# Two layers of four-way row and column scans: other partitions for the row positions, other engines for moving rows to columns, another place for a square root, other first and last stages

## The chip, the cores and the metric

The kernel runs on one core of one Trainium2 chip. Its time is the device time of one execution in microseconds (us); the median of the runs of a kernel is compared. All data are 32-bit floats. The engines are TensorE (PE in the profile; PEld are its weight loads), VectorE (DVE), ScalarE (ACT), GpSimd (POOL) and SyncE (SP), which issues nearly all DMA transfers.

## The reference

```python
# x: (32, 48, 64, 128) = batch, channels, rows H, columns W; two layers, each with its own weights
x = x + conv(gn(x), down_w, down_b, right_w, right_b, left_w, left_b)

def gn(v):      # 16 groups of 3 channels; mean and variance over group, H and W of one batch element
    return (v - m) / sqrt(s + 1e-5)

def step(w, b):  # conv1d: 48 -> 48 channels, 5 taps, padding 2
    nxt = inp + conv1d(carry, w, b)

# conv(): four scans, each over the result of the one before it
# down : rows 0 .. 63,    carry = finished row, conv along W
# up   : rows 63 .. 0,    the same weights as down
# right: columns 0 .. 127, carry = finished column, conv along H
# left : columns 127 .. 0
```

Each step of a scan needs the finished step before it, so a scan is a chain of 63 row steps or 127 column steps.

## The kernel before, in words

**Passes.** The 32 batch elements are worked in four groups of eight, `g` = 0 to 3, and in two layers, which makes eight passes, `n` = 0 to 7 (layer 0 of all groups, then layer 1). Names end in layer and group and, for scans, in d, u, r or l: `row_02d` is the down scan of layer 0, group 2. One large on-chip buffer, `arena`, holds the state of a pass; `stage` is four smaller buffers of 112 x 2048 elements for data on their way. DRAM buffers `xin` and `mid` hold the input of the two layers in the kernel's own order, so `mid` is the result of layer 0.

**Two layouts.** For row scans (view `rows`) a column W = 8k + e is split in e (8 values) and k (16 values). The 8 x 48 = 384 pairs of e and channel lie in three blocks `o` of 128 partitions, and a row has 16 x 8 (k, batch) elements in each. `PIECES` lists, for each e, which channels `c0:c1` lie in which block from which partition `p0` on. For column scans (view `cols`) the 48 channels lie on partitions 0 to 47 for even rows and 64 to 111 for odd ones (`SIDES`), with 32 row pairs, e, k and batch in the free dimension. `cols` begins where row 20 of `rows` begins, so rows and columns share most of `arena`.

**Scans.** A row step (`row_step`, L523) is nine products in PSUM (`PRODUCTS`, weights `wd`) and, for each block, one VectorE addition of PSUM, bias and input row (L542). A column step (`col_step`, L546) is done in two halves of the batch, each of three matmuls (L556 to L560) and one VectorE addition (L563).

**From rows to columns.** While the up scan runs, `hand_over` (L415) moves finished rows to `cols`. `HANDS` says after which row which rows go: at 48, 32, 16, 8 and 0. Odd rows go first, then even ones, and each has twelve pieces, one DMA each, on SP's queue.

**Side work.** Other work is cut into portions that the program issues at certain scan steps (`advance`): writing out the results of the pass before with the residual added (`drain`, `residual`), loading (`load_rows`) and scaling (`scale_rows`, L411, ScalarE) the rows of the next pass, restaging the input of the next group (`prepare`: `take_in`, `restage`), and the statistics of the group norms. `input_moments` takes the next group's input in 16 portions, `result_moments` takes the layer-0 result of the pass before from `mid` in 16 parts of eight batch elements each. Both load into three buffers, `spare`, that lie in rows 0 to 15 of `arena`, so the next pass's first rows can be loaded there only when both are done. ScalarE does the sums: per portion the sums (L196), the negated mean (L199), the squares of the deviations (L201). `scaling` (L218) makes scale and offset of a group from them, with two small matmuls, about ten VectorE operations and a square root on ScalarE (L273).

**Order.** `dma()` (L145) keeps all of SP's transfers in program order. Within an engine the framework's scheduler fixes the order by its own estimates when the kernel is built; `behind_steps` (L210) makes the operations of `scaling` come after the instructions kept in `mark`, the last matmul and the last VectorE addition of the scan steps issued so far. Each engine then works in its fixed order, and an instruction that waits holds up those behind it.

**First and last stage.** `prepare_first` (L357) loads all input of group 0 in 16 tiles (`stage` and free parts of `arena`, whose partitions 32 to 63 are set to zero before), computes statistics with VectorE, restages each tile to `xin` and reads the rows back. `last_residual` (L472) writes the result of the last pass in four parts of k, each in four quarters of the rows: residual loads, eight additions (L504) and sixteen writes per quarter. A part can begin when the left scan has passed its columns.

## Time and profile before

| what | value |
|---|---|
| median of 3 runs | 5443.56 us (5439.95 to 5454.95) |
| profiled execution | 5430.74 us, span 5429.0 us |
| TensorE busy | 4811.6 us, 89% of the span |
| VectorE, ScalarE, GpSimd busy | 2527.8, 1850.8, 1013.8 us |
| mean granted TensorE clock | 0.95 |
| chain that ended last, by engine | PE 79%, ACT 7%, SP's issues 5%, DMA 5% |

The profile is of one execution, and its times are in us from the start of the span, mean times of one instruction in ns. In the strips over 40 slices each digit is the busy share of a slice of 135.7 us in tenths. A row of the waits names the waiting engine and instruction, then what it waited for: us in total, times, the longest. A row of the timeline has start, duration, engine, line, operation, what is written and read, the count of equal instructions, and in brackets how long the engine was idle ahead and what ended that. A row of groups has busy time, then the mean in ns, then idle time before.

### The profile page before, as it was taken

Reading aid. Unit: us, or ns where it says so; the run is one execution under the profiler, and the core shown is the slowest. Engines: PE = TensorE matmul, PEld = TensorE weight load, DVE = VectorE, ACT = ScalarE, POOL = GpSimd, SP = SyncE. Lnnn points to the kernel's source line nnn. Section 1 sums busy time; section 2 is a strip of 40 time slices with the busy share of each in tenths; the row PEclk is TensorE's granted clock in tenths of the full one; section 3 lists DMA queues with packets and bytes.
Section 4 is the critical chain, followed back from the end, with each engine's and each line's share of the span. In section 5 each row is a group of like instructions: output and inputs, shape, how many; then the busy total and the mean of one; then the engine's idle time right before and its main releaser. Section 6 shows DMA issues by size and latency. Waiting matters only on the chain.

```text
span 5429.0 us, 103969 instructions
## 1 busy us (share of the span) xinstructions
PE 4811.6 (89%) x42592; PEld 4802.6 (88%) x42592; DVE 2527.8 (47%) x7394; ACT 1850.8 (34%) x4090; POOL 1013.8 (19%) x409
## 2 busy tenths in 40 slices
PE   2799999899199896399999989998999989998992
PEld 2799999899199896398999989998999989998992
DVE  6344554455045453154554545554554445544553
ACT  3604043134970409831945079041004120050000
POOL 2103122130041210130003100260005300260044
PEclk9899999999599998699999999999999999999996
DMA  8569648881397943686338744288007840189057
GB/s 174 113 84 219 124 83 174 152 205 36 59 235 110 219 89 65 133 188 99 69 54 182 118 84 75 55 193 126 2 1 163 139 73 1 37 200 120 1 63 101
DMA packets 827086, 599.91 MB, mean 111 GB/s; under 512 B 246544, under 2 KB 763408, under 8 KB 822000
## 3 DMA queue, kind: packets, MB, share of 16 engines
q1 hardware_dynamic: 810720, 590.73, 57.2%
q8 instruction: 335, 5.49, 0.5%
q10 hardware_dynamic: 15888, 2.52, 0.3%
q14 instruction: 143, 1.17, 0.1%
HBM read 341.40 MB, written 151.09 MB: 91 GB/s over the span
## 4 chain that ended last, share of the span: by engine, by line
PE 79%; ACT 7%; SPq 5%; DMA 5%; POOL 1%; DVE 1%; issue 1%; ACTq 0%; DVEq 0%; POOLq 0%
SPq L147 5%; ACT arena L201 3%; ACT arena L196 3%; PE row_13d L534 2%; PE row_10d L534 2%; PE row_01d L534 2%; PE row_00u L534 2%; PE row_12d L534 2%; PE row_12u L534 2%; PE row_01u L534 2%; PE row_10u L534 2%; PE row_03u L534 2%; PE row_11u L534 2%; PE row_13u L534 2%; PE row_02u L534 2%; PE row_02d L534 2%
## 5 line engine op out<-in xcount | busy, mean ns | idle before, releaser
L411 ACT ACTIVATE arena<-arena,offset_m,scale_m 128x128 f32<-128x128 f32 (+1 forms) x864 | 422.0, 587 | 1246.9 <-DMA arena<-mid 835.9
L196 ACT ACTIVATE arena<-arena,sides 112x256 f32<-112x256 f32 (+1 forms) x560 | 475.9, 856 | 914.2 <-DVE arena L563 463.0
L456 POOL TENSOR_TENSOR stage<-arena,stage 112x1024 f32<-112x1024 f32 x96 | 361.0, 3793 | 1443.2 <-DVE arena L563 1368.7
L447 POOL TENSOR_TENSOR stage<-arena,stage 112x2048 f32<-112x2048 f32 x64 | 289.2, 4532 | 1442.1 <-DMA stage<-xin 801.4
L411 ACT ACTIVATE arena<-arena,offset_x,scale_x 128x128 f32<-128x128 f32 (+1 forms) x848 | 414.1, 586 | 164.1 <-DMA arena<-xin 95.6
L201 ACT ACTIVATE arena<-arena,neg_m 112x256 f32<-112x256 f32 x512 | 379.8, 749 | 0.7
L341 POOL COPY stage<-stage 112x1024 f32<-112x1024 f32 x98 | 196.7, 2036 | 744.3 <-DMA stage<-in_x 550.7
L534 PE MATMUL row_03d<-arena,wd 128*128 128x128 f32 x1134 | 133.7, 282 | 130.4 <-DMA arena<-xin 118.7
L534 PEld LDWEIGHTS row_03d<-arena,wd 128*128 128x128 f32 x1134 | 132.4, 198 | 131.8 <-ACT arena L411 122.4
L534 PE MATMUL row_02d<-arena,wd 128*128 128x128 f32 x1134 | 134.6, 283 | 128.8 <-DMA arena<-xin 118.8
L534 PEld LDWEIGHTS row_02d<-arena,wd 128*128 128x128 f32 x1134 | 133.2, 199 | 130.2 <-ACT arena L411 122.5
L534 PE MATMUL row_00d<-arena,wd 128*128 128x128 f32 x1134 | 136.8, 286 | 47.5 <-DVE arena L542 38.2
L534 PEld LDWEIGHTS row_00d<-arena,wd 128*128 128x128 f32 x1134 | 135.0, 201 | 49.2 <-DVE arena L542 43.2
L542 DVE SCALAR_TENSOR_TENSOR arena<-row_03d,bd,arena 128x128 f32<-128x128 f32 x189 | 61.3, 349 | 202.9 <-DMA arena<-xin 130.1
L542 DVE SCALAR_TENSOR_TENSOR arena<-row_02d,bd,arena 128x128 f32<-128x128 f32 x189 | 61.3, 349 | 202.1 <-DMA arena<-xin 131.2
L273 ACT ACTIVATE std_x<-var_x 128x24 f32<-128x24 f32 x4 | 0.9, 222 | 420.8 <-DVE var_x L268 420.8
L534 PE MATMUL row_11u<-arena,wd 128*128 128x128 f32 x1134 | 129.7, 277 | 7.1 <-DVE arena L542 7.1
L534 PEld LDWEIGHTS row_11u<-arena,wd 128*128 128x128 f32 x1134 | 128.7, 194 | 7.7 <-DVE arena L542 7.7
L563 DVE SCALAR_TENSOR_TENSOR arena<-col_02r,bc,arena 112x128 f32<-112x128 f32 x254 | 89.1, 351 | 99.1 <-PE col_02r L560 99.1
L563 DVE SCALAR_TENSOR_TENSOR arena<-col_01r,bc,arena 112x128 f32<-112x128 f32 x254 | 89.1, 351 | 98.1 <-PE col_01r L560 98.1
L563 DVE SCALAR_TENSOR_TENSOR arena<-col_13r,bc,arena 112x128 f32<-112x128 f32 x254 | 89.1, 351 | 98.1 <-PE col_13r L560 98.1
L563 DVE SCALAR_TENSOR_TENSOR arena<-col_12r,bc,arena 112x128 f32<-112x128 f32 x254 | 89.1, 351 | 97.9 <-PE col_12r L560 97.9
(231 smaller groups left out, 13835.2 us busy)
## 6 DMA issues: line engine op xcount, KB each, us to landing
arena<-arena SPq DMA_DIRECT2D x288, 192.0 KB, 7.5
xin<-stage SPq DMA_DIRECT2D x128, 384.0 KB, 6.2
stage<-xin SPq DMA_DIRECT2D x128, 384.0 KB, 8.2
mid<-stage SPq DMA_DIRECT2D x128, 384.0 KB, 5.8
arena<-mid SPq DMA_DIRECT2D x128, 384.0 KB, 6.1
arena<-in_x SPq DMA_DIRECT2D x124, 384.0 KB, 9.3
stage<-in_x SPq DMA_DIRECT2D x100, 384.0 KB, 11.2
stage<-mid SPq DMA_DIRECT2D x96, 384.0 KB, 6.9
```

Of the source, the lines that this page charges most:

```text
L147: tc.keep_in_program_order(nc.sync.dma_start(dst, src))
L196: nc.scalar.activation(view, view, AF.Identity, scale=sides, accum_out=mo.sum[:, b, t : t + 1])
L201: nc.scalar.activation(view, view, AF.Square, bias=mo.neg[:, b, t : t + 1], accum_out=mo.dev2[:, b, t : t + 1],)
L273: nc.scalar.activation(std, var, AF.Sqrt)
L341: nc.gpsimd.tensor_copy(dst[:, r], src[:, r])
L411: nc.scalar.activation(args[0], args[0], AF.Identity, bias=args[2], scale=args[1])
L447: nc.gpsimd.tensor_tensor(nat, res, nat, ALU.add)
L456: nc.gpsimd.tensor_tensor(perm[:, t].rearrange("p (b k e) -> p b k e", b=GB, k=NK), cols[:, q + t].rearrange("p e k b -> p b k e"), nat[:, ...
L534: mark["pe"] = nc.tensor.matmul(ps[o][:, a:b], wd[:, i, o - NG * s - i + 1], prev[:, i, a + s * GB : b + s * GB], start=seen[o] == 1, stop ...
L542: mark["dve"] = nc.vector.scalar_tensor_tensor(dst[:, o], ps[o], bd[:, layer, o : o + 1], inp[:, o], ALU.add, ALU.add).ins
L563: mark["dve"] = nc.vector.scalar_tensor_tensor(dst, ps, bc[:, layer, way : way + 1], dst, ALU.add, ALU.add).ins
```

## The change

Four things are changed.

- **Positions and hand-over.** `PIECES` is written out. In each block the two whole pieces of 48 channels start at partition 0 or 64 (e = 0, 1, 3, 4, 6, 7), and e = 2 and e = 5 are split in three pieces of 16 channels at partitions 48 and 112. `hand_over` moves whole pieces with a ScalarE copy and the 16-wide ones with a DMA, so a hand has 12 copies and 12 transfers. `HANDS` has one more hand: rows 4 to 7 and 0 to 3 go apart.
- **Square root and statistics.** `collect` keeps its last instruction in `mark["act"]`, so that `scaling`, its square root (now L285) among the rest, is placed behind statistics already issued. The statistics are asked for at every third step of the right scan up to step 50, where it was every fourth up to 65.
- **First stage.** Tiles lie elsewhere; less is set to zero ahead of the loads; four restage buffers; from the seventh tile on GpSimd restages both halves; row loads stand between the writes of `xin` on SP instead of behind them. The row weights are put together in a buffer and copied to `wd` by GpSimd, since the permuted positions break the runs in which they were written.
- **Last stage.** The residual loads of `last_residual` are issued from ScalarE's queue instead of SP's.

ScalarE in the right and left scans of pass 1, before (`sum_x`: sums of the next input; `sum_m`: of the result in `mid`; `std_x`: the square root for the next pass):

```order
L196 ACTIVATE arena,sum_x_7873<-arena,sides 112x2048
L199 ACTIVATE neg_x_7874<-sum_x_7873 112x1
L201 ACTIVATE arena,dev_x_7875<-arena,neg_x_7874 112x2048
L273 ACTIVATE std_x_9144<-var_x_9140 128x24
L196 ACTIVATE arena,sum_m_8656<-arena,sides 112x256 x8
L199 ACTIVATE neg_m_8657<-sum_m_8656 112x8
L201 ACTIVATE arena,dev_m_8658<-arena,neg_m_8657 112x256 x8
```

and now:

```order
L207 ACTIVATE arena,sum_m_8559<-arena,sides 112x256 x8
L210 ACTIVATE neg_m_8560<-sum_m_8559 112x8
L212 ACTIVATE arena,dev_m_8561<-arena,neg_m_8560 112x256 x8
L285 ACTIVATE std_x_9435<-var_x_9431 128x24
L207 ACTIVATE arena,sum_m_8559<-arena,sides 112x256 x8
```

The square root stood ahead of all sixteen result parts; now eleven of them are ahead of it and five behind.

VectorE at the same place, the operations of `scaling` that follow the square root, between the additions of the left scan (L563), before:

```order
L268 TENSOR_SCALAR var_x_9140<-ps_x_8918 128x24
L270 COPY mean_x_9142<-ps_x_8918 128x24
L563 SCALAR_TENSOR_TENSOR arena<-col_01l_10307,bc,arena 112x32x4
L278 RECIPROCAL r_x_9245<-std_x_9144 128x24
L280 TENSOR_TENSOR t_x_9247<-var_x_9140,r_x_9245 128x24
L563 SCALAR_TENSOR_TENSOR arena<-col_01l_10312,bc,arena 112x32x4
```

and now, where `col_01l_11195` is the last addition of the left scan and `row_02d` the first of the next pass:

```order
L579 SCALAR_TENSOR_TENSOR arena<-col_01l_11195,bc,arena 112x32x4
L290 RECIPROCAL r_x_9536<-std_x_9435 128x24
L292 TENSOR_TENSOR t_x_9538<-var_x_9431,r_x_9536 128x24
L294 TENSOR_TENSOR t_x_9540<-t_x_9538,r_x_9536 128x24
L298 TENSOR_SCALAR t_x_9582<-t_x_9540 128x24
L300 TENSOR_TENSOR scale_x_9584<-r_x_9536,t_x_9582 128x24
L302 SCALAR_TENSOR_TENSOR offset_x_9586<-mean_x_9433,scale_x_9584 128x24
L558 SCALAR_TENSOR_TENSOR arena<-row_02d_11200,bd,arena 128x128
```

The reciprocal and what follows it stood within the left scan and now stand between its last step and the first step of the next pass.

```diff
@@ -48,7 +48,7 @@
 SHIFT = 20
 CH = 2
 RB = 8
-HANDS = {48: 64, 32: 48, 16: 32, 8: 16, 0: 8}
+HANDS = {48: 64, 32: 48, 16: 32, 8: 16, 4: 8, 0: 4}
 DOWN, RIGHT, LEFT = range(3)
 
 LOADS = ((0, 4), (4, 12), (12, 20), (20, 28), (28, 36), (36, 44), (44, 52), (52, 60), (60, 64))
@@ -67,17 +67,22 @@
 )
 
 
-def pieces():
-
-    for e in range(E8):
-        lo = C * e
-        while lo < C * (e + 1):
-            hi = min(C * (e + 1), (lo // FULL + 1) * FULL)
-            yield e, lo - C * e, hi - C * e, lo // FULL, lo % FULL
-            lo = hi
-
-
-PIECES = tuple(pieces())
+
+
+PIECES = (
+    (0, 0, 48, 0, 0),
+    (1, 0, 48, 0, 64),
+    (2, 0, 16, 0, 48),
+    (2, 16, 32, 0, 112),
+    (2, 32, 48, 1, 48),
+    (3, 0, 48, 1, 0),
+    (4, 0, 48, 1, 64),
+    (5, 0, 16, 1, 112),
+    (5, 16, 32, 2, 48),
+    (5, 32, 48, 2, 112),
+    (6, 0, 48, 2, 0),
+    (7, 0, 48, 2, 64),
+)
 
 
 @with_exitstack
@@ -147,27 +152,33 @@
         tc.keep_in_program_order(nc.sync.dma_start(dst, src))
 
 
-    nc.gpsimd.memset(arena[32:64, H * ROW + 7 * CH * PAIR :], 0.0)
-    nc.vector.memset(stage[32:64], 0.0)
-    nc.gpsimd.memset(wd, 0.0)
     nc.vector.memset(sides, 1.0)
     nc.vector.memset(sides[32:64], 0.0)
     nc.vector.memset(sides[32:48], 1.0)
 
-    def load_row_weights(layer: int, queue):
+    def load_row_weights(layer: int, queue, eng, buf):
+
 
 
         for j in range(TAPS):
             d, si = divmod(TAPS - 1 - j, 2)
             queue(taps[layer][:, j], w[SIDES[si], layer, DOWN, d, SIDES[0]])
+        buf = buf[:, 0 : NG * NG * FULL].rearrange("p (i m) -> p i m", i=NG)
+        eng.memset(buf, 0.0)
         for e, c0, c1, i, p0 in PIECES:
             to = C * (e - TAPS // 2) - FULL * (i - 1)
             queue(
-                wd[p0 : p0 + c1 - c0, i].rearrange("p o m -> p (o m)")[
-                    :, to : to + TAPS * C
-                ],
+                buf[p0 : p0 + c1 - c0, i, to : to + TAPS * C],
                 taps[layer][c0:c1].rearrange("c k m -> c (k m)"),
             )
+        for i in range(NG):
+            for lin in range(NG):
+                for e, c0, c1, o, p0 in PIECES:
+                    if o == (lin + i - 1) % NG:
+                        at = FULL * lin + C * e + c0 - FULL * o
+                        eng.tensor_copy(
+                            wd[:, i, lin, p0 : p0 + c1 - c0], buf[:, i, at : at + c1 - c0]
+                        )
 
     def load_col_weights(layer: int, queue):
         queue(wc, w[:, layer, RIGHT : LEFT + 1])
@@ -205,6 +216,7 @@
                 bias=mo.neg[:, b, t : t + 1],
                 accum_out=mo.dev2[:, b, t : t + 1],
             )
+        mark["act"] = nc.cur_bb.bb.instructions[-1]
 
     @contextmanager
     def behind_steps():
@@ -331,11 +343,11 @@
 
     def restage(g: int, j: int, nat):
 
-        perm = stage[:, 2 + j % 2]
+        perm = stage[:, (2 + j) % 4 if g == 0 else 2 + j % 2]
         src = nat.rearrange("p (b r k e) -> p r e k b", b=GB, r=CH, e=E8)
         dst = perm.rearrange("p (r e k b) -> p r e k b", r=CH, e=E8, k=NK)
         for r in range(CH):
-            if g == 0 and r:
+            if g == 0 and r and j < 6:
                 nc.scalar.copy(dst[:, r], src[:, r])
             else:
                 nc.gpsimd.tensor_copy(dst[:, r], src[:, r])
@@ -360,23 +372,26 @@
         size = CH * PAIR
         tiles = [stage[:, 0], stage[:, 1]]
         for j in range(2, NCH):
-            at = H * ROW + size * (j - 2 if j < 9 else j - 16)
+            at = H * ROW + size * (j - 9)
             tiles.append(arena[0:P, at : at + size])
-            eng = nc.vector if j % 2 else nc.gpsimd
-            eng.memset(tiles[-1][32:64], 0.0)
         at = H * ROW + 7 * size
         st = arena[0:P, at : at + GB * NCH * 6].rearrange(
             "p (b j k) -> p b j k", b=GB, j=NCH
         )
+        nc.vector.memset(arena[32:64, at:], 0.0)
         for j, nat in enumerate(tiles):
+            eng = nc.vector if j % 2 else nc.gpsimd
+            eng.memset(nat[32:64], 0.0)
             take_in(0, j, nat)
+        nc.vector.memset(stage[32:64, 2:4], 0.0)
         for j, nat in enumerate(tiles):
             by_batch = nat.rearrange("p (b n) -> p b n", b=GB)
             for b in range(GB):
                 nc.vector.bn_stats(st[:, b, j, :], by_batch[:, b])
             restage(0, j, nat)
-            if j % 2 == 0 and j // 2 < EARLY:
+            if j % 2:
                 load_rows(0, 0, j // 2)
+        load_rows(0, 0, len(LOADS) - 1)
         mo = Moments(1, 1, "x0")
         mv = stat_tile(2 * GB, "mv", "x0").rearrange("p (b k) -> p b k", k=2)
         for b in range(GB):
@@ -387,8 +402,6 @@
         for _ in scaling(mo, 0, 0):
             pass
         for j in range(len(LOADS)):
-            if j >= EARLY:
-                load_rows(0, 0, j)
             scale_rows(0, 0, j)
 
     def load_rows(layer: int, g: int, j: int):
@@ -419,7 +432,10 @@
             src = rows[:, h0 + r : h1 : 2].rearrange("p q o n -> o p q n")
             dst = cols[SIDES[r], qs].rearrange("p q e k b -> e p q (k b)")
             for e, c0, c1, o, p0 in PIECES:
-                dma(dst[e][c0:c1], src[o][p0 : p0 + c1 - c0])
+                if c1 - c0 == C:
+                    nc.scalar.copy(dst[e], src[o][p0 : p0 + C])
+                else:
+                    dma(dst[e][c0:c1], src[o][p0 : p0 + c1 - c0])
 
 
 
@@ -481,7 +497,7 @@
             nat = inputs[half].rearrange("p (q e n) -> p q e n", q=nq, e=E8)
             for r in range(2):
                 for e in range(E8):
-                    dma(
+                    nc.scalar.dma_start(
                         nat[SIDES[r], :, e],
                         src[r, e][
                             :,
@@ -589,16 +605,13 @@
             yield "left", v
 
 
-    load_row_weights(0, nc.scalar.dma_start)
+    load_row_weights(0, nc.scalar.dma_start, nc.gpsimd, arena)
     load_col_weights(0, nc.scalar.dma_start)
     nc.scalar.dma_start(mask_sb, mask)
     nc.scalar.dma_start(bc, bias)
     for e, c0, c1, o, p0 in PIECES:
         nc.scalar.dma_start(bd[p0 : p0 + c1 - c0, :, o], bias[c0:c1, :, DOWN])
-    nc.scalar.dma_start(
-        maskp.rearrange("p o m -> p (o m)").rearrange("p (e c) -> p e c", e=E8),
-        mask[:, 0:C].unsqueeze(1).to_broadcast([P, E8, C]),
-    )
+        nc.gpsimd.tensor_copy(maskp[:, o, p0 : p0 + c1 - c0], mask_sb[:, c0:c1])
     prepare_first()
 
     side = {}
@@ -650,10 +663,10 @@
                         side["prepare"] = prepare(nxt[1])
                     side["moments"] = all_moments(n)
                     if nxt and nxt[0] != layer:
-                        load_row_weights(nxt[0], dma)
+                        load_row_weights(nxt[0], dma, nc.gpsimd, arena)
                 if i % 6 == 2:
                     advance("prepare")
-                if i % 4 == 2 and i < 66 and n + 1 < NGRP:
+                if i % 3 == 2 and i <= 50 and n + 1 < NGRP:
                     advance("moments")
                 elif i % 8 == 2:
                     advance("moments")
```

## The prediction

> **What bounds the kernel now.** I read the page first, for how much of the span PE works and where it does not; then PE's waits, which give the price of each hole; then what releases the three kinds of holes.
>
> ```profile
> PE 4811.6 (89%) x42592; PEld 4802.6 (88%) x42592; DVE 2527.8 (47%) x7394; ACT 1850.8 (34%) x4090; POOL 1013.8 (19%) x409
> PE   2799999899199896399999989998999989998992
> ACT  3604043134970409831945079041004120050000
> PE row_02d L534 <- DMA arena<-xin: 118.8, 1, 118.8
> PE row_03d L534 <- DMA arena<-xin: 118.7, 1, 118.7
> PE col_01r L556 <- DMA arena<-arena: 15.0, 1, 15.0
> PE col_03r L556 <- DMA arena<-arena: 13.4, 1, 13.4
> 273.48 126.66 PE row_00u L534 x1134
> 1026.47 0.74 PE L556 MATMUL col_01r<-arena,wc 112*112 112x128 f32 x2 [15.03 <-DMA arena<-arena]
> 1369.64 0.38 PE L560 MATMUL col_01l<-arena,wc 112*112 112x124 f32 x2
> ```
>
> The span is 5429.0 us, the profiled execution took 5430.74. TensorE is at 9 tenths nearly everywhere: the scans are a serial chain of matmul and VectorE addition, and a step costs 126.66/63 = 2.01 us in the row scans and (1370.02 - 1026.47)/254 = 1.35 us in the column scans. Neither step is touched, so the change can only move the holes. There are four kinds: the start (the first slice reads 2), the end (the last reads 2), two boundaries of 119 us (the 1s and 3s in the middle; passes 1 to 2 and 2 to 3), and eight hand-overs, of which the longest and the shortest wait are shown.
>
> **The boundaries.** Here is what ScalarE does in pass 1, between the first column step (call it R = 1026.47) and the next pass:
>
> ```profile
> ACT std_x L273 <- DVE var_x L268: 420.8, 4, 122.2
> 1167.37 0.19 ACT L201 ACTIVATION_READ_ACCUMULATOR arena<-arena,neg_x 112x1 f32 x1
> 1289.76 0.22 ACT L273 ACTIVATE std_x<-var_x 128x24 f32<-128x24 f32 x1 [122.20 <-DVE var_x L268]
> 1289.89 0.75 ACT L196 ACTIVATE arena<-arena,sides 112x256 f32<-112x256 f32 x1
> 1482.27 0.19 ACT L201 ACTIVATION_READ_ACCUMULATOR arena<-arena,neg_m 112x1 f32 x1
> 1488.81 1.22 PE L534 MATMUL row_02d<-arena,wd 128*128 128x128 f32 x4 [118.79 <-DMA arena<-xin]
> 1546.16 87.28 PE row_02d L534 x766
> 2387.16 8.05 PE row_03u L534 x72
> ```
>
> Input statistics end at 1167.56, which is R+141. The square root is next in ScalarE's queue, and its operand comes 122.20 us later. Behind it stand sixteen parts of result statistics, 1289.89 to 1482.46, 192.6 us or 12.04 each. The left scan has ended at 1370.02, 112 us before them. The first rows of the next pass share the statistics' buffers, so their loads come last.
>
> The change puts that square root after 11 of the 16 parts and asks for the statistics every third step, not every fourth. ScalarE then has no reason to stand still. Even if the input statistics do not end sooner, the results run from R+141, plus some 7 us for their first load, for 192.6 us: to R+341, against the scan's end at R+343.5. The hole as such closes. What is late next: the reciprocal and the five operations behind it now stand on VectorE after the last left step, so no scaling of the next rows can start before; then the first rows must be scaled.
>
> ```profile
> L411 ACT ACTIVATE arena<-arena,offset_x,scale_x 128x64 f32<-128x64 f32 x24 | 9.5, 489 | 3.1 <-DMA arena<-xin 3.1
> L411 ACT ACTIVATE arena<-arena,offset_x,scale_x 128x128 f32<-128x128 f32 x30 | 15.4, 614 | 0.0
> ```
>
> Six operations of some 0.3 us make 2 us; the first four rows take 9.5 us; the next eight 24 x 0.51 = 12.3, less four row steps of 2.01 that run meanwhile: 2 + 9.5 + 12.3 - 8.0 = 16, and 2 for the cold start, 18 in all. Before, a boundary cost 118.8 and then a down scan of 1633.44 - 1488.81 = 144.6 instead of 126.7, together 136.7 (the other one likewise). Gain 2 x 119 = 238. Bounds: at the top 246, if the scalings pipeline by 4 us more; at the bottom 118, if each part waits for its loads on SP behind the restaging of the next input, 16 us a part instead of 12.04, so 16 x 4 less a little, 60 us late per boundary. A row for such waits is there, for the input parts:
>
> ```profile
> ACT arena L196 <- DMA arena<-in_x: 318.5, 31, 182.0
> ```
>
> **The hand-overs.** Row results go to the column layout by 24 transfers per hand, all issued by SP.
>
> ```profile
> L147 SPq DMA_DIRECT2D arena<-arena x25: 582/602/615, 1013.7 to 1029.6; - x25
> DMA to landing us min/median/max: 2.0/2.3/2.6
> L201 ACT ACTIVATE arena<-arena,neg_x 112x2048 f32<-112x2048 f32 x48 | 96.1, 2003 | 1.6
> L201 ACT ACTIVATE arena<-arena,neg_m 112x256 f32<-112x256 f32 x512 | 379.8, 749 | 0.7
> L339 ACT COPY stage<-arena 112x1024 f32<-112x1024 f32 x14 | 28.1, 2020 | 15.4 <-DMA xin<-stage 15.4
> ```
>
> 25 issues in 15.9 us are one per 0.66: the last hand takes 24 x 0.66 = 15.8 us, and that, less the issues for the odd rows that begin before the last row ends and with a landing behind it, is the wait of 13.4 to 15.0 us that PE shows. Now 12 of the 24 are ScalarE copies. SP needs 12 x 0.66 = 7.9 us, and the piece that the second column step reads (the third of the even rows) is issued at 8 x 0.66 = 5.3 and lands at 7.6; the step before it, which reads only copied columns, is done by then: hole about 6.3. The copies have no row here. In the last hand each has 256 elements a partition: 250 ns by the widest statistics row (2003 x 256/2048), 505 by the one kind of copy that ScalarE makes now, with strided operands (2020 x 256/1024), 749 by the row of the same size; twelve make 3.0, 6.1 or 9.0 us. I take the middle, since that row is a copy; the first column needs only two of the twelve, so the copies lie beside SP's issues. Gain 8 x (14.1 - 6.3) = 62. Bounds: 96 if the hole is 2 us, one landing; 16 if copies and pieces together keep it at 12. The 72 copies of a pass (36 of 1024 elements, 12 of 512, 24 of 256) make 97 us by the copy row, beside an up scan of 126.7 in which PE waits for nothing of ScalarE's.
>
> **The start.**
>
> ```profile
> 0.00:18.00 18.00, 0.00 (x0) 0.00 (x0) 13.79 (x8) 0.00 (x0) 15.15 (x14) 1.00 0.47 87
> 18.00:79.00 61.00, 0.00 (x0) 0.00 (x0) 46.14 (x125) 6.61 (x4) 3.73 (x2) 1.00 1.09 209
> 95.00:137.00 42.00, 34.54 (x261) 33.68 (x262) 13.66 (x42) 36.04 (x54) 12.06 (x6) 0.88 0.70 178
> 137.00:185.00 48.00, 13.75 (x110) 12.97 (x108) 5.85 (x18) 26.84 (x33) 14.06 (x7) 0.67 0.92 201
> 2.51 6.88 DVE L151 MEMSET stage<- 32x8192 f32 x1 [2.51 <-issue]
> 94.93 10.29 PE L534 MATMUL row_00d<-arena,wd 128*128 128x128 f32 x72 [5.72 <-POOL arena L409]
> ```
>
> (Columns after the length: PE, PEld, DVE, ACT, POOL busy, PE clock, DMA share, GB/s.) Input loads run at full DMA share from 18 to 79 us; before 18 they stand at 0.47, behind memsets of the tiles they fill, of which the first takes 6.88. With memsets a quarter as long ahead of them they are full from about 5: 0.47 x 18 + 1.09 x 61 = 75 us of transfers, at 1.09 in 69 us, so they end 9 or 10 us sooner, and everything up to the first matmul with them. The first down scan runs from 94.93 to 273.48, 178.6 us, of which 51.9 are not steps; 42 of them lie between 95 and 185, where rows wait behind 22 writes of restaged input on SP. With reads interleaved they wait only for ScalarE's scalings: 24 x 0.61 = 14.7 us for eight rows against 16.1 of steps, so 12 us remain, mostly the first rows. Gain 10 + 40 = 50; bounds 20 (in the first loads nothing, half of the stall) and 58.
>
> **The end.**
>
> ```profile
> 5203.31 16.49 POOL L504 TENSOR_TENSOR stage<-arena 112x256 f32<-112x256 f32 x16 [316.76 <-DVE arena L563]
> 5211.60 9.09 SPq L147 DMA_DIRECT2D out<-stage  x16
> 5331.10 0.37 PE L560 MATMUL col_13l<-arena,wc 112*112 112x124 f32 x2
> 5374.09 15.29 SPq L147 DMA_DIRECT2D stage<-mid  x16
> 5389.43 37.07 SPq L147 DMA_DIRECT2D out<-stage  x48
> L504 DVE TENSOR_TENSOR stage<-arena x10: 601/1483/1491, 5374.1 to 5404.9; 112x256 f32<-112x256 f32 x10
> q1 hardware_dynamic: 164864, 20.47, 72.3%
> q10 hardware_dynamic: 12800, 1.57, 4.6%
> ```
>
> PE ends at 5331.5 and the span 97.5 us later: SP has fallen behind, since it issues the loads of residuals too. These go to ScalarE's queue, which is idle there. Then a quarter part costs SP 9.1 us of writes and POOL 16.49/2 = 8.25 us of additions; four of them take some 37 us, and the left scan frees a part in 32 x 1.35 = 43, so parts 3 to 1 are done with the scan. Behind it lies part 0: four quarters at five VectorE additions of 1.48, 30 us, and the last writes, 5 to 12: a tail of 42. Gain 55; bounds 12 (one part still late by a whole cycle of 43) and 68.
>
> By the Trainium skill ("DMA: Bandwidth & Descriptors", section "Issuing engines are not separate DMA queues") all issuers share the same 16 DMA engines, and a second issuer saves only the time of issue, usually little. The trace does not refute it; by it the gain of this part could be near zero, which is the first rival.
>
> **The sum.** 238 + 62 + 50 + 55 = 405 off 5430.7 gives 5026 for a profiled execution. The median of the runs shown, 5443.56, lies 12.8 above the profiled one; I add that: **5040**. At all lower bounds, 118 + 16 + 20 + 12 = 166, it is 5278; at all upper, 468, it is 4976.
>
> **The rivals.**
>
> 1. *The DMA engines bound the end* (15%). Over the 226 us from 5203 the two queues' packets took 72.3 + 4.6 = 76.9% of 16 engines, 174 us. Starting at 5211.6 they could not end before 5386: tail 54, time 5052; with the whole of today's tail kept, 5095. For it: the share is high for a stage in which SP issues one transfer after the other. Against it: it is not 1, so the engines have room that the issuing leaves.
> 2. *The small pieces keep the hand-over late* (12%). Twelve DMAs still follow the last row, and a landing of 2.3 us comes after the last that matters; if the wait ends with the last one and copies slow it, the hole is 12: 5040 + 8 x 5.8 = 5086.
> 3. *Result statistics are paced by SP* (10%). They start early but their loads stand behind the input's restaging: 60 us late at both boundaries, 5040 + 120 = 5160.
> 4. *The other side: result statistics without overlap* (3%). The results share three buffers and SP's queue with the restaging of the next input. If each load waits until the part before is done and SP has gone through the restaging, a part costs load and work one after the other. At 26 us a part (12.04 of work, and some 14 of waiting, against the 318.5/31 = 10.3 of the input row) they end at R+141+7+416 = R+564, 220 behind the scan; with the 18 that makes 238 a boundary, 102 more than now, and the loss of 204 exceeds the other three gains (167): 5443 + 37 = 5480. It decides from 25 us a part on. For it: 31 waits of input parts in the row above. Against it: while the results run now, back to back, a part takes 12.04, and the earlier request leaves SP more steps ahead of them.
>
> That the change does not do what it says is excluded for the square root: the order of ScalarE shows it behind eleven parts.
>
> **How the numbers follow.** The forecast has 60%, the rivals 15, 12, 10 and 3. The range 4980 to 5140 holds the forecast's own spread (boundaries 8 up, hand-overs 34 up, start and end some 20 either way), rivals 1 and 2, and leaves out the third and the fourth and both tails. A measurement of this kernel tells 0.3%, 16 us, from no change. All cases but the fourth are far on the faster side: faster 0.95, same 0.02, slower 0.03.
>
> **What would show it.** PE's waits for xin at row_02d and row_03d should be under 25 us instead of 119, and std_x should wait on ScalarE for little; what holds PE there should be ScalarE's scalings or the offset of VectorE. Waits at the col_..r steps should be near 6 us, eight times. PE should start near 85 and the first down scan should end near 224. PE's end should lie some 42 us before the span's end, with POOL never idle for over 5 us in it before part 0. Wrong would be: result statistics on ScalarE that end after the left scan, by waits for DMA arena<-mid; col waits of 12 and more; a last stage in which DMA share stays at 0.9 while SP idles.

## The result

The changed kernel takes 5083.43 us (median of 4 runs, 5067.92 to 5099.47); the kernel before takes 5441.76 (median of 4 runs). The ratio is 0.934, 95% interval 0.930 to 0.937: 358 us or 6.6% faster. Forecast were 5040 and a range of 4980 to 5140. The sign, the range and the largest term held; 43 us of the forecast gain did not come.

### The profile page after: what moved, and what is told of

The parts are those of the page before. It is cut to its first block, busy times and chain, and to the rows that moved or that the text cites. A ratio compares the mean times of both kernels' runs of the same rounds, so it can differ in the third digit from the quotient of the medians.

```text
span 5072.3 us, 104799 instructions
## 1 busy us (share of the span) xinstructions
PE 4806.6 (95%) x42592; PEld 4794.2 (95%) x42592; DVE 2534.4 (50%) x7396; ACT 2272.9 (45%) x4656; POOL 1049.0 (21%) x504
## 5 line engine op out<-in xcount | busy, mean ns | idle before, releaser
L436 ACT COPY arena<-arena 48x1024 f32<-48x1024 f32 (+2 forms) x576 | 437.1, 759 | 767.8 <-DVE arena L558 760.7
L579 DVE SCALAR_TENSOR_TENSOR arena<-col_11r,bc,arena 112x128 f32<-112x128 f32 x254 | 89.0, 351 | 87.7 <-PE col_11r L576 84.4
L579 DVE SCALAR_TENSOR_TENSOR arena<-col_03r,bc,arena 112x128 f32<-112x128 f32 x254 | 89.0, 351 | 86.7 <-PE col_03r L576 83.0
L520 POOL TENSOR_TENSOR stage<-arena 112x256 f32<-112x256 f32 x54 | 58.3, 1118 | 356.6 <-DVE arena L579 328.4
```

What stands on the lines that cost most here:

```text
L436: nc.scalar.copy(dst[e], src[o][p0 : p0 + C])
L520: eng.tensor_tensor(perm[:, :, t].rearrange("p b (k e) -> p b k e", k=kn), cols[:, no * i + t, :, ks].rearrange("p e k b -> p b k e"), nat ...
L579: mark["dve"] = nc.vector.scalar_tensor_tensor(dst, ps, bc[:, layer, way : way + 1], dst, ALU.add, ALU.add).ins
```

## The profile after, stage by stage

The engines' busy times and two strips of the page of the changed kernel (span 5072.3 us, execution 5074.23):

```profile
PE 4806.6 (95%) x42592; PEld 4794.2 (95%) x42592; DVE 2534.4 (50%) x7396; ACT 2272.9 (45%) x4656; POOL 1049.0 (21%) x504
PE   1999999999999999999999999999999999998994
ACT  2645214489735897359453891533005510143000
```

TensorE's work is the same, and it now fills 95% of the span: the two dips in the middle of its strip are gone. Of what PE waited for, the rows that the change bears on (us in total, times, longest):

```profile
PE col_13r L572 <- DMA arena<-arena: 17.5, 1, 17.5
PE row_02d L550 <- ACT arena L424: 8.1, 3, 5.1
PE row_03d L550 <- ACT arena L424: 8.0, 3, 5.0
PE col_02r L572 <- DMA arena<-arena: 3.0, 1, 3.0
PE col_12r L572 <- ACT arena L436: 0.5, 1, 0.5
```

The two waits of 119 us are down to 8, and behind them now stand ScalarE's scalings. In pass 1 ScalarE has its last result part done at 1284.44, 28 us before the left scan ends, and then itself waits for the coefficients:

```profile
ACT arena L424 <- DVE offset_x L302: 30.2, 1, 30.2
```

The hand-overs' waits are 3 us, but one of 17.5 has come in the last pass that was in no forecast. From the first and last matmul of each scan:

| stage, us | before | after | gain | forecast |
|---|---|---|---|---|
| first matmul | 94.9 | 106.1 | -11 | 10 |
| first down scan beyond its 126.8 | 51.7 | 6.5 | 45 | 40 |
| eight hand-overs: holes and right scans | 1496.0 | 1419.0 | 77 | 62 |
| boundaries 1 to 2 and 2 to 3 | 274 | 38 | 236 | 238 |
| last matmul to the end of the span | 97.5 | 69.7 | 28 | 55 |

A boundary is its hole, the excess of the down scan behind it over 126.8 and that of the left scan ahead of it over 171.5: before 136.6 + 137.4 = 274, after 17.0 + 15.3 + 5.7 = 38. These gains are 375 us; the spans differ by 357. The other 18 lie mostly in row scans of layer 1: 8 in the up scan of pass 5 (137.4 before, 145.6 after), which took 147.3 in a second profile of the kernel before and so differs by execution, and some 3 in each of the down scans of passes 5 to 7, for which no cause is shown.

## Experiments

Every run but one is the changed kernel with the edit shown. Beside them the kernel before took 5454.6 to 5458.5 us (medians), 13 to 17 more than beside the changed kernel, so between them and the changed kernel's 5083.43 a difference of some 15 us says nothing by itself; the holes in the profiles say more.

**The boundaries: which half of the edit closed them?** Two runs undo one half each.

```diff
-        mark["act"] = nc.cur_bb.bb.instructions[-1]        # e1_mark_undone
-                if i % 3 == 2 and i <= 50 and n + 1 < NGRP:  # e1_pace_undone
+                if i % 4 == 2 and i < 66 and n + 1 < NGRP:
```

> The square root is put back ahead of the sixteen result parts on ScalarE; statistics still asked for at every third step. Theory (both halves are needed: the place of the root and the earlier request, which moves the root's operand on VectorE from left half-step 134 to 52): ScalarE stands still from the end of the input statistics (about R+141, R being the first column step) to left half-step 52 (R+172+35 = R+207), then works 192.6 us, to R+400, 56 us behind the left scan; with what follows (24 us before) each of the two boundaries costs some 80 us instead of 17 to 21: 120 us more in all, about 5200. Rival 1 (the place of the root alone closed the hole): 136 us a boundary as before, 235 more, 5318. Rival 2 (the earlier request alone closed it): no change, 5083.

> Statistics asked for at every fourth step again; the root still goes behind statistics already issued, which now are five result parts, and its operand comes at left half-step 129. Theory: ScalarE does five parts, waits until about R+172+87 = R+259, then does eleven parts of 12.04, to R+392, 48 us behind the scan; boundaries of some 72 us, 105 more in all, about 5190. Rival 1 (the place of the root alone closed the hole): no change, 5083. Rival 2 (the request alone): as before the change, 5318.

Measured: 5215.99 us (5210.72 to 5221.27) with the mark undone, 5218.83 (5216.92 to 5220.75) with the pace undone: 133 and 135 above the changed kernel, where 120 and 105 were expected and the rivals said 0 and 235. ScalarE's wait for the root in pass 1 and PE's holes, with the mark undone:

```profile
ACT std_x L284 <- DVE var_x L279: 92.6, 1, 92.6
PE row_02d L549 <- DMA arena<-xin: 67.3, 1, 67.3
PE row_03d L549 <- DMA arena<-xin: 67.2, 1, 67.2
```

and with the pace undone:

```profile
ACT std_x L285 <- DVE var_x L280: 41.0, 1, 41.0
PE row_02d L550 <- DMA arena<-xin: 55.2, 1, 55.2
PE row_03d L550 <- DMA arena<-xin: 55.1, 1, 55.1
```

In the changed kernel std_x waits for nothing in this pass. So neither half does it alone: the earlier request moves the root's operand from left half-step (half of a column step) 134 to 52, and the mark lets ScalarE work meanwhile. A third run asks whether the root stands too late, since the coefficients now come behind the last left step. It is taken from a kernel whose first residual loads are on SP (below).

```diff
-        mark["act"] = nc.cur_bb.bb.instructions[-1]
+        if mo.T == 2 or t < 5:     # behind five result parts
+            mark["act"] = nc.cur_bb.bb.instructions[-1]
```

> As the run with only the first residual loads on SP, and the square root of passes 1 and 2 is placed behind five result parts, not eleven. Its operand comes at left half-step 52 (R+207), when ScalarE has just done five parts (R+148+60), so it stands nowhere; reciprocal to offset then lie at left half-step 154 instead of behind the last step. Theory (what is left of a boundary is the coefficients behind the scan and the scaling of the first rows behind them, and VectorE's small operations take 4.4 us each where GpSimd's additions have begun): the result parts still end at R+325, the first rows can be scaled before the scan ends at R+345, the waits of 5 to 22 us at row_02d and row_03d and the slow first steps behind them go: 15 to 17 us per boundary, 30 to 50 in all: 5071 - 35 = 5036, with less spread between runs. Rival (the loads of the first rows end last, not the coefficients): boundaries stay at 15 us, 5071.

Measured: 5094.84 us (5080.79 to 5097.21), against 5071.11 for its base: slower than theory and rival had it. PE waits for the loads of the first rows, as the rival said. The run's waits in pass 1 and at the row scan:

```profile
ACT std_x L286 <- DVE var_x L281: 28.6, 1, 28.6
PE row_02d L552 <- DMA arena<-xin: 6.5, 1, 6.5
```

ScalarE had done five parts some 24 us sooner than I reckoned (the earlier request shortened the input statistics too), stood 28.6 us before the root, and so ended the results with the scan (1315.97 and 1316.36) instead of 28 us before it as in the changed kernel; the first rows' loads come behind that. The hole with the down scan behind it costs 6.5 + 149.1 - 126.8 = 29 us, not 17 to 19. An estimate from these numbers: the root would stand well behind seven or eight parts (28.6/12.04 = 2.4 more); that was not tried.

**The hand-overs.** All pieces by SP, new positions and hands kept:

```diff
-                if c1 - c0 == C:
-                    nc.scalar.copy(dst[e], src[o][p0 : p0 + C])
-                else:
-                    dma(dst[e][c0:c1], src[o][p0 : p0 + c1 - c0])
+                dma(dst[e][c0:c1], src[o][p0 : p0 + c1 - c0])
```

> All twelve pieces of a hand go by SP again, from the new positions and with the extra hand at row 4. Theory (SP's 24 issues of 0.66 us set the hole, whatever the hand's size): 13 to 15 us before the second or third column step at seven passes instead of the 3 us that are left now, and more in the last pass, where SP's issues are late already: 8 x 11 = 88, and some 10 for the last pass: about 5180. Rival (the smaller last hand made the gain): holes stay near 3 us, 5085.

Measured: 5311.53 us (5304.73 to 5316.71), 228 more than the changed kernel. PE's longest and shortest wait of the eight, and two between:

```profile
PE col_13r L569 <- DMA arena<-arena: 45.3, 1, 45.3
PE col_01r L569 <- DMA arena<-arena: 34.2, 1, 34.2
PE col_00r L569 <- DMA arena<-arena: 33.0, 1, 33.0
PE col_10r L569 <- DMA arena<-arena: 31.6, 1, 31.6
```

The copies are what closes the hole, as the theory said, but its size was wrong: I had 14 us from the last hand alone, and SP carries a backlog. SP's hand-over transfers of pass 1, first in the kernel before, up to the end of the last row (1011.45) and from there to the first column step, then the same in this run (1000.42):

```profile
912.52 99.11 SPq L147 DMA_DIRECT2D arena<-arena  x72
1011.02 15.90 SPq L147 DMA_DIRECT2D arena<-arena  x24
```

```profile
901.47 99.03 SPq L152 DMA_DIRECT2D arena<-arena  x84
999.89 35.17 SPq L152 DMA_DIRECT2D arena<-arena  x53
```

The kernel before has ten pieces for odd and ten for even rows, since e = 2 and e = 5 are split in two; with five hands a pass has 100 transfers. 72 are out when the last row ends, and the first column step waits for the 91st: 19 issues of 0.66 and a landing of 2.6 make its 15 us. In this run a pass has 144, twelve pieces and six hands; 84 are out, and the step waits for the 133rd: 49 issues and a landing of 2.0, 34 us. So without the copies the new positions and the extra hand are a loss; which of the two costs more, no run tells. With the copies a pass has 72 transfers, 63 of them out when the last row ends, and SP just keeps step. The copies themselves (1024, 256 and 512 elements) cost

```profile
L436 ACT COPY arena<-arena 48x1024 f32<-48x1024 f32 x288 | 300.6, 1044 | 708.5 <-DVE arena L558 705.2
L436 ACT COPY arena<-arena 48x256 f32<-48x256 f32 x192 | 77.4, 403 | 30.9 <-DVE arena L558 28.2
L436 ACT COPY arena<-arena 48x512 f32<-48x512 f32 x96 | 59.2, 617 | 28.4 <-DVE arena L558 27.3
```

about 0.2 us and 0.83 ns an element: 55 us a pass, where I had put 97 by the strided copy.

**The last stage and the hole at col_13r.** Four runs.

The edits are shortened, each with the run that it belongs to:

```diff
-                    nc.scalar.dma_start(      # residual loads of last_residual
+                    dma(                      # e3_tail_sp: all; e3_first_sp: only part 3
-                if i % 2 and part:            # e3_no_loads, with part 3 on SP
-                    load(part - 1, half)
-                            nq * half : nq * (half + 1),           # e3_thin_loads, parts 2 to 0
+                            nq * half + nq - 1 : nq * (half + 1),
```

> The residual loads of the last stage are issued by SP again. Theory (transfers of SP and ScalarE share eight completion counters in turn, so that a waiting residual load on ScalarE's queue holds up SP's hand-over in the last pass): the hole of 17.5 us at col_13r goes to about 3; the tail goes back from 70 to some 97 us, since SP issues 48 transfers per half again: net 5083 + 27 - 15 = 5095. Rival 1 (the 16 DMA engines bound the tail): tail stays near 70, 5068. Rival 2 (the 17.5 us come from the extra hand or the copies): hole stays, 5110.

> Of the residual loads only the first 32 (part 3), which are issued around the last hand-over, go back to SP; parts 2 to 0 stay on ScalarE's queue. Theory (a residual load that waits on ScalarE's queue for the end of the up scan holds the counter that SP's next hand-over transfer needs): the hole of 17.5 us at col_13r goes to about 3, the tail stays near 70: 5083 - 14 = 5069. Rival (the hole has another cause, such as the copies): no change, 5083.

> As the run with only the first loads on SP, and the residual loads of parts 2 to 0 are left out, so that these parts add stale residuals. Theory (SP's writes stand waiting for residual loads with which they share counters; the tail's additions and writes alone keep up with the scan): POOL's cycle per half falls from 27 to about 18 us and below the scan's 21.6, the tail to 35 to 42 us, some 30 less. Rival (writes or additions themselves are too slow): tail stays over 60.

> As the run with only the first residual loads on SP; the loads of parts 2 to 0 keep their number, queue and waits, but each moves only one of its sixteen row pairs, so these parts add residuals that are mostly stale. Theory (SP's writes wait for completion counters that are held by residual loads which themselves wait for POOL's additions; the data of the loads matter little): the tail stays above 60 us, near the 72 with whole loads. Rival (the shared DMA engines are the limit): with a sixteenth of the data the tail falls to near the 42 us of the run without loads.

| run | time, us | hole at col_13r | last matmul to end |
|---|---|---|---|
| changed kernel | 5083.43 | 17.5 | 69.7 |
| all loads on SP | 5097.49 (5079.31 to 5109.22) | 3.1 | 93.6 |
| part 3 on SP | 5071.11 (5053.59 to 5082.69) | 3.3 | 71.9 |
| same, other loads left out | 5035.8 (one run) | 3.2 | 41.8 |
| same, other loads a sixteenth | 5058.5 (one run) | 3.6 | 73.3 |

The hole and the long tail have one mechanism, and it is in the program. The eight counters that tell the end of a transfer are given in turn to the transfers of SP and of ScalarE's queue, and a transfer waits until the one that had its counter before is done. Two transfers of the last pass as built, the first of ScalarE's residual loads into rows of `arena` and the next of SP's hand-over transfers that has the same counter, with what each waits for and what counts its end (DMAHW0 to 7 are the counters):

```
L500 DMA arena<-mid_89 48x16x32 [waits DMAHW5_49,PE_49,Activation_49; counted by DMAHW5_49]
L152 DMA arena<-arena 16x2x128 [waits DMAHW5_49,DVE_49,Activation_49; counted by DMAHW5_49]
```

The load goes into rows that the up scan and ScalarE's copies still read, and is issued at 4644.22, behind the scan's end at 4642. Until its end SP's transfer waits, though it reads nothing of it, and with it all that SP has to issue behind: SP goes on at 4646.73 with 24 hand-over transfers to do. SP's waits in the changed kernel, first from 4600 to 4670 and then in the last stage:

```profile
SPq L152 <- DMA arena<-mid: 14.3, 1, 14.3
...
SPq L152 <- DMA stage<-mid: 24.0, 5, 8.9
SPq L152 <- DMA arena<-mid: 21.8, 3, 7.7
```

None of SP's writes reads what these loads bring; 46 us of SP's last stage go to them. The run with a sixteenth of the data settles what they cost: over 4870 to 5110 the packets on ScalarE's queue fall from the first row, of the run with part 3 on SP, to the second, and the tail does not:

```profile
q10 hardware_dynamic: 88064, 11.02, 30.7%
```

```profile
q10 hardware_dynamic: 18944, 2.17, 6.2%
```

It is not the data, so not the DMA engines, but the waiting. Without the loads GpSimd begins the last part 0.5 us after the last matmul, and the tail is 41.8. That it is just the 42 that I had reckoned is partly luck: VectorE's additions take some 5.4 us a quarter, not 7.4, and the rest is waits for writes. The fifth run gives both queues the same order of work: even rows' writes and loads on SP, odd rows' on ScalarE's queue (part 3 on SP, the root behind five parts as above).

```diff
+            queues = (dma, dma if part == 3 else nc.scalar.dma_start)   # of the loads: even, odd rows
-                        if part == 0 and r:                             # of the writes
+                        if r:
```

> As the run with the root behind five parts, and in the last stage SP has the writes and loads of the even rows, ScalarE's queue those of the odd rows (the first 32 loads on SP). Theory (a load that waits for POOL must not hold a counter that earlier writes need; with both queues in the same order the waits come in the order in which POOL releases them, and each queue issues 24 transfers per half, 13 us): the cycle per half falls from 27 to some 19 to 22 us, the tail from 72 to 45 to 50: 25 off the run before: 5011. Rival (the DMA engines, or the writes' landing, hold the cycle): tail stays near 70.

Measured: 5090.84 us (5080.50 to 5096.15), tail 61.8 against 71.2 for its base, so 9 us of the 25; the total moves by 4, and both have the dearer boundaries. SP's longest wait for a load fell from 8.9 to the 2.5 of

```profile
SPq L152 <- DMA out<-stage: 26.3, 84, 1.9
SPq L152 <- DMA stage<-mid: 25.1, 24, 2.5
```

but there are many: with 48 transfers a half and eight counters, the landing of each counts. How far below 62 this order could go stays open.

**The first stage.** The small transfers of weights go between the input loads on SP instead of ahead of them on ScalarE's queue; once alone, once with part 3 on SP. And the kernel before, unchanged, is profiled again.

```diff
-    load_row_weights(0, nc.scalar.dma_start, nc.gpsimd, arena)   # and bias, mask, column weights
             take_in(0, j, nat)
+            for args in small[2 * j : 2 * j + 2]:
+                dma(*args)
```

> The 32 small weight, bias and mask transfers of the first stage are issued by SP between the input loads, two after each tile, instead of by ScalarE's queue ahead of them. Theory (the input loads wait for the small transfers' completion counters until 24 us): input loads flow from about 4 us on, the last lands 12 us sooner than at 88 us, PE starts at about 94 instead of 106: 5071. Rival 1 (transfer rate alone bounds the input): the loads end at the same time, PE at 106, 5083. Rival 2 (small transfers between the loads slow them): PE later than 106.

> The first residual loads on SP and the weights between the input loads, together. Theory: the two gains add, 14 + 12: 5057, with the measurement's spread of some 15. Rival: the small transfers only move the wait to the first rows: 5069.

> The kernel before, unchanged, profiled again. In its first profile the later input loads came at one per 1.75 us, in nine profiles of kernels with the new first stage at one per 2.16 to 2.40. Theory (the rate differs between executions or chips and not by the kernel): 2.2 or more here too, PE's first row step at 100 or later instead of 94.9. Rival (the new first stage slows the loads itself): 1.75 again, first row step near 95.

Measured: 5074.87 us (5069.73 to 5088.75) and 5082.65 (5066.28 to 5085.49): neither differs from its base (5083.43, 5071.11) by more than the runs do. The first of them issues its input loads sooner, as these rows of SP's timeline show, of the changed kernel and of the run:

```profile
3.68 14.66 SPq L152 DMA_DIRECT2D stage<-in_x  x4
19.40 10.77 SPq L152 DMA_DIRECT2D arena<-in_x  x9
```

```profile
5.61 0.94 SPq L152 DMA_DIRECT2D stage<-in_x  x2
8.92 2.95 SPq L152 DMA_DIRECT2D arena<-in_x  x2
```

but PE starts at 105.4 instead of 106.1, and the last input load lands at 87.4 instead of 88.1: from the 16th landing to the 32nd a load took 2.40 us, against 2.30 in the changed kernel. So the run does not tell its theory from rival 1 by itself. SP's first input load is issued at 3.68 in the changed kernel and at 9.42 in the kernel before, yet the first four are out at 18.3 and 18.8. The row of the kernel before, and what SP waits for up to 30 us in the changed kernel:

```profile
9.42 9.40 SPq L147 DMA_DIRECT2D stage<-in_x  x4
```

```profile
SPq L152 <- DMA bd<-in_b: 6.1, 5, 3.7
SPq L152 <- DMA arena<-taps: 4.5, 1, 4.5
```

The rate of the later loads is what the executions differ in. Input loads issued from 40 to 65 us and their median time to landing, in the first profile of the kernel before, in the second, and in the changed kernel:

```profile
arena<-in_x SPq DMA_DIRECT2D x14, 384.0 KB, 13.1
```

```profile
arena<-in_x SPq DMA_DIRECT2D x12, 384.0 KB, 16.5
```

```profile
arena<-in_x SPq DMA_DIRECT2D x12, 384.0 KB, 16.7
```

The second profile of the kernel before has PE's first row step at 104.76, not 94.93, and a span of 5452.5: against it the changed kernel starts 1 us later, not 11. Its input ended at 88.7, the changed kernel's at 88.1, at nearly the same rate (2.27 and 2.30). Over all profiles a later load took 1.75 to 2.40 us, and the start moved with it (99.2 at 1.99, 102.5 at 2.16, 111.9 at 2.40). What sets the rate of an execution is not shown. At the same rate (2.40, 2.38) the two runs of the weights start 6 to 9 us sooner than their likes (111.9 and 110.6 at 2.40 and 2.39); that much of the theory may hold, though the times do not show it.

The best run that does all the work, part 3 on SP, has the ratio 0.929 to the kernel before, interval 0.926 to 0.932; the changed kernel has 0.934, 0.930 to 0.937. The intervals overlap, so a gain in time is not shown; that the hole went is.

## Why the prediction was right, and where it was not

- **Boundaries: right.** 238 forecast, 236 measured. Results end before the scan does, and what is left is the coefficients, the scaling of the first rows and a slow first part of the down scan, 17 and 15 us against 18. The results end sooner than I had them, at R+318 in pass 1 and not R+341, since the earlier request ends the input statistics at R+115, not R+141. The step "has no reason to stand still" needed both halves, as the two undone runs show. One thing was missed: the statistics' small operations in the left scan cost it 5.7 us in pass 2.
- **Hand-overs: cause right, working wrong.** SP's issues make the hole and the copies close it. But a hand of the kernel before is 20 transfers, not 24, since it has ten pieces and not twelve, and none of the last hand is issued beside the last row: the 15 us of pass 1 are eight issues left of the hand before, eleven of the last, and a landing. That my 15.8 less something came out near was luck, and the backlog that it left out is what the run without copies showed. For the changed kernel I reckoned a hole of 6.3 us from the third even piece; it is 0.5 before the first step, which needs ScalarE's copies only, and some 2 to 3 before the third. Three of the last twelve transfers are out when the last row ends, so that piece lands 5.8 us after it in pass 1, not 7.6, and two steps run meanwhile, not one. Seven of the hand-overs together gain more than the eight of the forecast. The copies took half of what I put.
- **The step that failed** is the tail's "parts 3 to 1 are done with the scan". That is, I counted SP's writes and POOL's additions, 18.5 us per half against 21.6 of the scan; the half took about 27, because SP's writes wait for ScalarE's loads. GpSimd ended part 1 at 5025, 23 us behind the scan, and the tail was 70, not 42. Rival 1 gave times of 5052 to 5095 that fit, but not by its cause: the DMA engines were no limit, as the thin loads show. The Trainium skill ("DMA: Bandwidth & Descriptors", section "Issuing engines are not separate DMA queues") warns that a second issuer saves little; here it saved 28 of 55 us, and the reason that the rest was lost is not the shared engines that the section names.
- **The same coupling made the hole at col_13r**, 15 us more than its likes. I had priced the loads moved to ScalarE's queue as free there, "which is idle", and looked at no queue that they could hold up.
- **Start: half wrong.** The stall of the first down scan fell by 45 (40 forecast); no run undoes that edit alone. The 10 us from earlier loads did not come, for three reasons. By my own numbers 69 us from 5 on end at 74, 5 sooner than 79 and not 10. The memsets had held the first load alone; the next ones waited for the small transfers of weights and bias, and still do. And I took 1.09 of DMA share over 61 us as a fixed rate, but it was that execution's; at the rate of the second profile of the kernel before the input ends only 0.5 sooner, and the first step follows it by 18.0 us instead of 16.1.
- **The sum:** of the 405, the tail lacks 27, col_13r takes 15, the first matmul 21, the boundaries 2 and other row scans 18; the other hand-overs add 30 and the first down scan 5. That is 357, as in the profiles; the median lies 43 above the forecast.
- **Rivals 2, 3 and 4** did not come: the hole is not 12, the result parts took 12 us each, and nothing lay behind the scan.

## What to carry to other kernels

Moving transfers to an idle engine's queue frees issue time, but where the framework hands completion counters round over all queues, a transfer that waits for its data holds up the next ones of the other queue too: issue a load that will wait where its wait is due anyway, as with part 3 on SP. A queue that is off this round was not tried. An instruction that waits in a fixed order costs what stands behind it; moving it behind ready work and making its operand earlier are two edits, and either alone gives less than half. Smaller last portions, of more pieces, cost time where SP moved them all and fell behind; what the extra hand alone gains beside the copies was not tested.

## What was not expected of the hardware

VectorE's small operations took 24 times their usual time beside GpSimd. In the changed kernel the coefficients at boundary 2 to 3 take 0.18 us each, and GpSimd's additions begin behind them, at 1944.44:

```profile
1940.09 0.18 DVE L292 TENSOR_TENSOR t_x<-var_x,r_x 128x24 f32<-128x24 f32 x1
1940.31 0.18 DVE L294 TENSOR_TENSOR t_x<-t_x,r_x 128x24 f32<-128x24 f32 x1
1940.52 0.18 DVE L298 TENSOR_SCALAR t_x<-t_x 128x24 f32<-128x24 f32 x1
```

In the run with weights and part 3 moved, the additions began with them. The first rows are VectorE's, the last is GpSimd's:

```profile
1939.83 4.51 DVE L296 TENSOR_TENSOR t_x<-var_x,r_x 128x24 f32<-128x24 f32 x1
1944.37 4.42 DVE L298 TENSOR_TENSOR t_x<-t_x,r_x 128x24 f32<-128x24 f32 x1
1948.83 4.41 DVE L302 TENSOR_SCALAR t_x<-t_x 128x24 f32<-128x24 f32 x1
1953.27 4.42 DVE L304 TENSOR_TENSOR scale_x<-r_x,t_x 128x24 f32<-128x24 f32 x1
```

```profile
1939.81 17.84 POOL L480 TENSOR_TENSOR stage<-arena,stage 112x2048 f32<-112x2048 f32 x4 [138.65 <-DVE r_x L294]
```

Four operations of 0.18 us wait out four additions of 4.46 each, and the boundary costs 22.1 us at row_03d instead of 5.0. The Trainium skill ("SBUF — State Buffer", section "Who interferes with whom") says that VectorE and GpSimd share a pair of ports, taken by whoever issues first for a whole instruction; the trace agrees, by these rows. Eight profiles have the root behind eleven parts, with two such boundaries each; three of the sixteen show it, for 13 to 17 us: here, with all loads on SP, and with the weights moved alone. So it depends on when GpSimd's first addition begins, and may be a part of the spread between runs; that was not tested by itself.
